# Streamed attention weights issued by GpSimd instead of SyncE, and the feed-forward bias added by an accumulating DMA

## The chip, the core and the metric

The kernel runs on one core of one Trainium2 chip. A core has TensorE (PE in the profile, with PEld for its weight loads), VectorE (DVE), ScalarE (ACT), GpSimd (POOL) and SyncE (SP). Each of them works through its own list of instructions in order. SP computes nothing here: it issues DMAs. ACT issues a few as well. The bytes of all of them are moved by the same 16 DMA engines of the core.

The metric is the device time of one execution in microseconds; lower is better.

## The reference

A "macaron" block works on x, 2 x 1024 tokens of 1024 float32 each: half a feed-forward network, attention, half a feed-forward network.

```python
x = x + 0.5 * ffn(layernorm(x), gate_w, base_w, base_b, lora_A, lora_B)
x = x + attn(layernorm(x), Wq, Wk, Wv, Wo)
x = x + 0.5 * ffn(layernorm(x), gate_w, base_w, base_b, lora_A, lora_B)

def ffn(x):                     # the same weights both times
    logits = x @ gate_w.T                      # 8 experts
    w, sel = top_k(logits, 2); w = softmax(w)
    result = x @ base_w.T + base_b             # 1024 -> 1024
    result += 2 * sum over the two experts of w * (x @ lora_A[e].T) @ lora_B[e].T   # rank 16
    return result

def attn(x):                    # 32 heads of 32, 8 key/value heads, RoPE, causal
    q, k, v = x @ Wq, x @ Wk, x @ Wv
    return softmax(mask(rope(q) @ rope(k).T / sqrt(32))) @ v @ Wo
```

What the change touches is `+ base_b` (scaled by 0.5, since half of the network's result is added) and the way in which Wq, Wk, Wv and Wo come to SBUF.

## The kernel before, in words

The 2048 tokens are 16 tiles of 128 (one token in a partition), 8 for each batch. A tile passes four stages: `stage_a1` (layernorm, first feed-forward network), `stage_a2` (projections to k and v, and to q in two halves), `stage_c1` (output projection after the attention, in two halves) and `stage_c2` (layernorm, second feed-forward network, store). Between a2 and c1 stands the attention: for each key/value head and each block of keys, `unit_s1` computes scores once for the row maximum, and `unit_s2` computes them again in transposed form, takes the exponential on ACT, and feeds the product with v and the row sums (`av_batch`).

All dense products split a float32 operand into two float16 halves and take three products for one (lines 358, 359 and 360, in `dense`). The feed-forward weights stay in SBUF (`wb`, `ag`). The attention's weights don't fit beside them: at the start they are scaled, split and written to DRAM (`wstr`, by `prep_stream`), five chunks (k and v together; q in two; o in two) of two halves, 1 MB each in the split form. From there every tile streams them in again. Three SBUF buffers `ws0` to `ws2` hold one half each. `prefetch(ci)`, called at the end of a dense product for the next chunk in the list `order`, issues the two loads of that chunk; half number n goes into the buffer that half number n - 3 has left, so it waits until the last matmul on half n - 3 has been done. In the kernel before, SP issues these loads at line 370. SP also issues the DMA transposes of the normalized rows (`tt`, line 314), of k (`kts`, line 501) and of q (`qt`, line 553), and loads and stores x.

In `ffn`, lines 393 to 395 add the bias to the residual tile `xt` in two halves of 512 columns on GpSimd. `xt` has been read by the layernorm's activation (line 349) at that time; the scaled result of the matmuls is added to it later, on DVE, half by half (line 444). The bias lies in SBUF in all 128 partitions (`bb`, loaded at line 793, halved on ACT at line 233).

GpSimd's other work: the variance's power -1/2 in `layernorm` (lines 335 and 337), products with the sine table in `rope` (475 and 479), the causal masks of the two kinds of score blocks (585 on `sm`, 720 on `p`), the low half of the attention's result (673), and in the preparation a quarter of the splitting (192) and small scalars (177, 187).

The order of the dense stages among the attention's units is written out by hand (`SEQS`, `NORMAL`, `plan`, `step`); the order of the instructions on every engine's list is then set by the framework's scheduler, which places an instruction by the time at which it reckons it ready. The instructions of one engine, DMA issues among them, start in that order.

Of the kernel before, what the change touches and what calls it, by code (L numbers as in the profile page):

```python
# [9 lines left out]
FP = mybir.dt.float32  # L10
# [3 lines left out]
ALU = mybir.AluOpType  # L14
AX = mybir.AxisListType

B, T, D = 2, 1024, 1024
NH, NKV, DH, GRP = 32, 8, 32, 4
E, R = 8, 16
P = 128  # L20
KB = D // P
# [18 lines left out]
def kernel(  # L40
# [16 lines left out]
    nc = tc.nc  # L57
# [3 lines left out]
    const = ctx.enter_context(tc.tile_pool(name="const", bufs=1))  # L61
    wres = ctx.enter_context(tc.tile_pool(name="wres", bufs=1))
    small = ctx.enter_context(tc.tile_pool(name="small", bufs=SB))
# [4 lines left out]
    dram = ctx.enter_context(tc.tile_pool(name="dram", bufs=1, space=bass.MemoryType.DRAM))  # L68
# [17 lines left out]
        out=cmask, in_=cmask, compare_op=ALU.is_ge, fill=-NEG, base=0,  # L86
# [6 lines left out]
        out=tri, in_=tri, compare_op=ALU.is_gt, fill=0.0, base=0,  # L93
# [7 lines left out]
    nc.gpsimd.memset(ones, 1.0)  # L101
    cosT = const.tile([P, TPB, DH // 2], FP)
    sinT = const.tile([P, TPB, DH], FP)
    bb = const.tile([P, D], FP)

    qst = [stat.tile([P, NH, P], HP, name=f"qst{j}") for j in range(2)]
    kst = stat.tile([P, NKV, P], HP)
# [9 lines left out]
    def pin(ins):  # L117

        if pinned[0]:
            tc.keep_in_program_order(ins)  # L120
# [3 lines left out]
    def load_x(t):  # L124
        xt = xp.tile([P, D], FP, name="xt")
        pin(nc.sync.dma_start(out=xt, in_=late["x"] if t == LATE and late else xf[bass.ts(t, P), :]))
        xts[t] = xt
# [8 lines left out]
    wstr = dram.tile([5, 2, P, 2, KB // 2, 512], HP)  # L136
# [88 lines left out]
    def prep_lora(st):  # L225
        c = const.tile([P, 2], FP, name="sl")
        nc.vector.tensor_copy(c[:, 0:1], S["l",])
        nc.vector.scalar_tensor_tensor(c[:, 1:2], INV["b", 0], S["l",], S["b", 1], ALU.mult, ALU.mult)
        for n in range(2):
            h, s = bass.ts(n, 512), c[:, n : n + 1]  # L230
            nc.scalar.activation(lbh[:, h], st[:, h], AF.Copy, scale=s)
            nc.vector.scalar_tensor_tensor(lbl[:, h], st[:, h], s, lbh[:, h], ALU.mult, ALU.subtract)
        nc.scalar.mul(bb, bb, 0.5)

    KV = [wk_in, wv_in]
    CHUNKS = {
# [8 lines left out]
    def stage(ci, h, slot, eng):  # L245
        staged[ci, h] = piece(slot, CHUNKS[ci][0], h, eng)
# [81 lines left out]
    def layernorm(xt, n=1):  # L328
        st = small.tile([P, 2, 6], FP, name="bst")
        for c in range(2):  # L330
            nc.vector.bn_stats(st[:, c, :], xt[:, bass.ts(c, 512)])
        mv = small.tile([P, 2], FP, name="mv")
        nc.vector.bn_aggr(mv, st.rearrange("p a b -> p (a b)"))
        ve = small.tile([P, 1], FP, name="ve")
        nc.gpsimd.tensor_scalar(ve, mv[:, 1:2], EPS, None, ALU.add)
        r = small.tile([P, 1], FP, name="r")
        nc.gpsimd.tensor_tensor(r, ve, mhalf, ALU.pow)
        n1 = small.tile([P, 1], FP, name="n1")
        nc.vector.scalar_tensor_tensor(n1, ve, r, r, ALU.mult, ALU.mult)
        nc.vector.tensor_scalar(n1, n1, -0.5 * XS, 1.5 * XS, ALU.mult, ALU.add)  # L340
        rs = small.tile([P, 1], FP, name="rs")
        nc.vector.tensor_tensor(rs, n1, r, ALU.mult)
        nb = small.tile([P, 1], FP, name="nb")
        nc.vector.scalar_tensor_tensor(nb, mv[:, 0:1], -1.0, rs, ALU.mult, ALU.mult)
        xn = fpool.tile([P, D], FP, name="xn")
        sp = Split(n)
        for i in range(n):
            c = bass.ts(i, D // n)
            nc.scalar.activation(xn[:, c], xt[:, c], AF.Identity, bias=nb, scale=rs)  # L349
            sp.add(xn)  # L350
        return sp

    def dense(ps, tt, wsel, n=512, last=True):

        for k in range(KB):
            wh, wl = wsel(k)
            th, tl = tt.high(k), tt.low(k)
            nc.tensor.matmul(ps, lhsT=th, rhs=wh, start=(k == 0), stop=False)  # L358
            nc.tensor.matmul(ps, lhsT=th, rhs=wl, start=False, stop=False)  # L359
            nc.tensor.matmul(ps, lhsT=tl, rhs=wh, start=False, stop=(last and k == KB - 1))  # L360
            if k % 2 == 1:
                yield
# [3 lines left out]
    def prefetch(ci):  # L366
        for h in range(2):
            w = wss[turn[0] % 3]
            turn[0] += 1
            nc.sync.dma_start(out=w, in_=wstr[ci, h])  # L370
            stream.append((ci, w))

    order = deque()
# [16 lines left out]
    def ffn(xt, tt, done):  # L390
        psa = p_dense.tile([P, 512], FP, name="pd")
        yield from dense(psa[:, 0 : P + E], tt, lambda k: (ag[:, 0, k, :], ag[:, 1, k, :]))
        for n in range(2):
            c = bass.ts(n, 512)
            nc.gpsimd.tensor_tensor(xt[:, c], xt[:, c], bb[:, c], ALU.add)  # L395

        lg = small.tile([P, E], FP, name="lg")
        nc.scalar.activation(lg, psa[:, P : P + E], AF.Copy, scale=S["cg"])
        nv = small.tile([P, 1], FP, name="nv")
        nc.vector.tensor_reduce(nv, lg, AX.X, ALU.max, negate=True)  # L400
        ex = small.tile([P, E], FP, name="ex")
        nc.scalar.activation(ex, lg, AF.Exp, bias=nv)
        fe = lg.unsqueeze(1).to_broadcast([P, E, E])
        ee = lg.unsqueeze(2).to_broadcast([P, E, E])
        lw = small.tile([P, E, R], FP, name="lw", bufs=1)
        gt, eq = lw[:, :, 0:E], lw[:, :, E : 2 * E]
        nc.vector.tensor_tensor(gt, fe, ee, ALU.is_gt)
        nc.vector.tensor_tensor(eq, fe, ee, ALU.is_equal)
        nc.vector.tensor_tensor(eq, eq, tri, ALU.mult)
        nc.vector.tensor_tensor(gt, gt, eq, ALU.add)  # L410
        rk = small.tile([P, E], FP, name="rk")
        nc.vector.tensor_reduce(rk, gt, AX.X, ALU.add)
        nc.vector.scalar_tensor_tensor(ex, rk, 1.5, ex, ALU.is_lt, ALU.mult)
        sm = small.tile([P, 1], FP, name="sm")
        nc.vector.tensor_reduce(sm, ex, AX.X, ALU.add)
        nc.vector.reciprocal(sm, sm)
        nc.vector.tensor_scalar(ex, ex, sm, S["inva2"], ALU.mult, ALU.mult)
        nc.vector.tensor_tensor(
            lw, psa[:, 0:P].rearrange("p (e r) -> p e r", r=R),
            ex.unsqueeze(2).to_broadcast([P, E, R]), ALU.mult,  # L420
        )
        yield True
        psb = [None, None]
        lh = ll = None
        for n in range(2):
            ps = p_dense.tile([P, 512], FP, name="pd")
            psb[n] = ps
            yield from dense(
                ps, tt, lambda k: (wb[:, n, 0, k, :], wb[:, n, 1, k, :]), last=False
            )  # L430
            if n == 0:
                pst = p_s1.tile([P, GRP, P], FP, name="s1")[:, 0, :]
                nc.tensor.transpose(pst, lw.rearrange("p e r -> p (e r)"), ident)
                lh = small.tile([P, P], HP, name="lh", bufs=LB)
                ll = small.tile([P, P], HP, name="ll", bufs=LB)
                nc.scalar.copy(lh, pst)
                nc.vector.tensor_tensor(ll, pst, lh, ALU.subtract)
                yield
            c = bass.ts(n, 512)
            nc.tensor.matmul(ps, lhsT=lh, rhs=lbh[:, c], start=False, stop=False)  # L440
            nc.tensor.matmul(ps, lhsT=lh, rhs=lbl[:, c], start=False, stop=False)
            nc.tensor.matmul(ps, lhsT=ll, rhs=lbh[:, c], start=False, stop=True)
            yield
            nc.vector.scalar_tensor_tensor(xt[:, c], ps, S["uf", n], xt[:, c], ALU.mult, ALU.add)  # L444
            done(n)
            if n == 0:
                yield True

    def stage_a1(t):
        tt = layernorm(xts[t])  # L450
        yield

        def done(n):
            if n == 1:
                Ts["x2", t] = layernorm(xts[t])
                if t == LATE:
                    late["x"] = dram.tile([P, D], FP, name="xlate")
                    nc.sync.dma_start(out=late["x"], in_=xts.pop(t))

        yield from ffn(xts[t], tt, done)  # L460
        yield True
# [310 lines left out]
    for h in range(2):  # L772
        for src, c in ((a_in, slice(0, P)), (g_in, slice(P, P + E))):
            pin(
                nc.sync.dma_start(
                    out=agst[:, h, :, c],
                    in_=src[h * (D // 2) : (h + 1) * (D // 2), :].rearrange("(k p) n -> p k n", p=P),
# [4 lines left out]
    pin(nc.sync.dma_start(out=lst, in_=lb_in))  # L782
    b0 = [piece(h - 2, [wb_in[:, 0:512]], h, nc.sync) for h in range(2)]
    load_x(1)
    a1 = [stage_a1(t) for t in range(3)]
    next(a1[0])
    prep_gate(gst)
# [2 lines left out]
    prep_base(0, b0)  # L790
    load_x(2)
    next(a1[1])
    pin(nc.sync.dma_start(out=bb, in_=bias_in.partition_broadcast(P)))
    stage(2, 0, 0, nc.scalar)
    stage(2, 1, 1, nc.scalar)
    prep_base(1, b1)
# [243 lines left out]
```

## Time and profile before

| | |
|---|---|
| median of 3 runs | 1523.7 us (1520.88 to 1530.89) |
| profiled execution | 1528.72 us, of which its span is 1527.0 us |
| granted TensorE clock, mean | 0.974 |
| PE busy | 1404.1 us, 92% of the span |
| DVE busy | 1139.7 us, 75% |
| ACT busy | 755.5 us, 49% |
| POOL busy | 450.1 us, 29% |
| DMA, mean | 175 GB/s |

The span runs from the first to the last instruction of the program. Busy times of engines overlap; a busy PE is not PE at its peak, because matmuls are pipelined and their ends are modelled. Issuing a DMA is not counted as busy time. A row of the form "SPq L370 <- PE pd L360: t, n, m" says that SP's queue stood at an instruction of line 370 and waited until a matmul of line 360 released it: t us in n times, at most m us. "To landing" is the time from the start of a DMA's issue until all its data is there.

### The profile page before, as it was taken

The numbers are of one execution on the slowest core, as the hardware profiler recorded it, in microseconds if no ns is written. First come the engines' busy times: TensorE is split into PE (matmuls) and PEld (weight loads), VectorE is DVE, ScalarE is ACT, GpSimd is POOL, SyncE is SP. The second block draws the span as 40 slices with busy tenths as digits, with TensorE's granted clock in tenths as the row PEclk, the third lists the DMA queues.
The fourth block names the chain that finished last, engine by engine and source line by source line (L and its number), as shares of the span: only waits on it lengthen the run. The fifth ranks groups of instructions, "written<-read, shape, count | busy, mean of one in ns | idle before, by whom it ended". The sixth has DMA issues, their size and how long they took to land.

```text
span 1527.0 us, 35303 instructions
## 1 busy us (share of the span) xinstructions
PE 1404.1 (92%) x14548; PEld 783.4 (51%) x14548; DVE 1139.7 (75%) x2420; ACT 755.5 (49%) x1374; POOL 450.1 (29%) x665
## 2 busy tenths in 40 slices
PE   3686897989999999999999899999999999989998
PEld 2243444455555555555654445555555555556544
DVE  6877656686968879789764767886869788689753
ACT  7564334453545545456552434553545455556631
POOL 3443213432323233122121323332323232312231
PEclk9798999989999999999999999999999999999999
DMA  9957697658575581853646769857383853834651
GB/s 274 333 156 204 115 237 205 206 127 264 123 238 137 153 254 31 235 160 69 209 160 191 216 161 272 202 160 234 72 294 69 237 147 70 271 69 98 133 170 45
DMA packets 293075, 267.30 MB, mean 175 GB/s; under 512 B 258480, under 2 KB 261552, under 8 KB 272432
## 3 DMA queue, kind: packets, MB, share of 16 engines
q1 hardware_dynamic: 289360, 252.45, 60.5%
q10 hardware_dynamic: 3552, 12.58, 2.3%
q8 instruction: 114, 1.87, 0.5%
q14 instruction: 49, 0.40, 0.1%
HBM read 181.63 MB, written 20.45 MB: 132 GB/s over the span
## 4 chain that ended last, share of the span: by engine, by line
PE 65%; DVE 13%; DMA 13%; ACT 3%; issue 2%; POOL 1%; SPq 1%; DVEq 0%; ACTq 0%; POOLq 0%
PE pd L358 13%; PE pd L359 13%; PE pd L360 13%; PE av L657 10%; PE s L712 7%; PE s L573 6%; DMA ws<-wstr 6%; DMA qt<-qst 5%; DVE mx L590 3%; DVE pair L636 1%; DVE ws L195 1%; DMA tt<-hl 1%; DVE o L666 1%; ACT p L718 1%; DVE hl L311 1%
## 5 line engine op out<-in xcount | busy, mean ns | idle before, releaser
L718 ACT ACTIVATE p<-s,cs 128x512 f32<-128x512 f32 x576 | 382.3, 688 | 291.2 <-PE s L712 284.1
L590 DVE TENSOR_REDUCE mx<-s 128x4 f32<-128x512 f32 x480 | 313.6, 675 | 68.3 <-PE s L573 46.8
L358 PE MATMUL pd<-ws,tt 128*128 128x512 f16 x592 | 226.8, 383 | 20.9 <-DMA ws<-wstr 16.8
L636 DVE TENSOR_TENSOR pair<-p,p 128x512 f32<-128x512 f32 x256 | 185.6, 727 | 72.6 <-ACT p L718 34.8
L573 PE MATMUL s<-kts,qt 96*128 96x128 f16 x2304 | 217.0, 222 | 23.8 <-DMA qt<-qst 17.8
L359 PE MATMUL pd<-ws,tt 128*128 128x512 f16 x592 | 226.3, 382 | 0.0
L712 PE MATMUL s<-qt,kts 128*128 128x512 f16 x576 | 210.7, 386 | 16.4 <-DMA qt<-qst 11.6
L360 PE MATMUL pd<-ws,tt 128*128 128x512 f16 x592 | 225.4, 382 | 0.0
L573 PEld LDWEIGHTS <-qt 96*128 96x128 f16 x2304 | 165.5, 99 | 116.4 <-issue 30.4
L359 PEld LDWEIGHTS <-tt 128*128 128x128 f16 x1360 | 135.6, 100 | 141.9 <-issue 31.3
L358 PEld LDWEIGHTS <-tt 128*128 128x128 f16 x1360 | 135.6, 100 | 135.5 <-issue 16.7
L358 PE MATMUL pd<-wb,tt 128*128 128x512 f16 x512 | 199.0, 389 | 5.0 <-DVE xt L444 5.0
L360 PEld LDWEIGHTS <-tt 128*128 128x128 f16 x1360 | 135.3, 99 | 131.5 <-issue 10.2
L359 PE MATMUL pd<-wb,tt 128*128 128x512 f16 x512 | 198.0, 387 | 0.5 <-DVE wb L195 0.5
L360 PE MATMUL pd<-wb,tt 128*128 128x512 f16 x512 | 197.7, 386 | 0.0
L657 PE MATMUL av<-p,va 128*32 128x128 f32 x4608 | 166.8, 278 | 4.8 <-ACT o L664 2.5
L720 POOL TENSOR_SCALAR_AFFINE_SELECT p<-p 128x512 f32<-128x512 f32 x128 | 89.0, 698 | 274.7 <-ACT p L718 264.4
L673 POOL TENSOR_TENSOR tt<-o,tt 128x128 f16<-128x128 f32 x128 | 70.5, 551 | 279.6 <-ACT tt L672 279.3
L657 PEld LDWEIGHTS av<-p,va 128*32 128x32 f32 x4608 | 115.5, 110 | 68.3 <-issue 53.4
L666 DVE RECIPROCAL o<-o 128x128 f32<-128x128 f32 x128 | 120.6, 942 | 24.9 <-ACT o L664 24.9
L585 POOL TENSOR_SCALAR_AFFINE_SELECT sm<-sm 128x512 f32<-128x512 f32 x96 | 66.4, 692 | 203.9 <-ACT sm L584 202.1
L395 POOL TENSOR_TENSOR xt<-xt,bb 128x512 f32<-128x512 f32 x64 | 92.3, 1464 | 59.6 <-ACT xn L349 59.4
(177 smaller groups left out, 1808.2 us busy)
## 6 DMA issues: line engine op xcount, KB each, us to landing
ws<-wstr SPq DMA_DIRECT2D x148, 1024.0 KB, 5.9
wstr<-ws ACTq DMA_DIRECT2D x9, 1024.0 KB, 6.1
xt<-in_x_dram SPq DMA_DIRECT2D x16, 512.0 KB, 3.8
out_dram<-xt SPq DMA_DIRECT2D x15, 512.0 KB, 2.8
ws<-in_wb_dram SPq DMA_DIRECT2D x2, 1024.0 KB, 8.0
qst<-in_wb_dram SPq DMA_DIRECT2D x2, 1024.0 KB, 6.8
st<-in_wo_dram SPq DMA_DIRECT2D x2, 1024.0 KB, 10.0
kts<-in_wo_dram SPq DMA_DIRECT2D x2, 1024.0 KB, 12.0
```

Source lines behind the costliest of these rows:

```text
L358: nc.tensor.matmul(ps, lhsT=th, rhs=wh, start=(k == 0), stop=False)
L359: nc.tensor.matmul(ps, lhsT=th, rhs=wl, start=False, stop=False)
L360: nc.tensor.matmul(ps, lhsT=tl, rhs=wh, start=False, stop=(last and k == KB - 1))
L395: nc.gpsimd.tensor_tensor(xt[:, c], xt[:, c], bb[:, c], ALU.add)
L573: nc.tensor.matmul(ps[:, h, :], lhsT=q[0 : 3 * DH, h, :], rhs=KT[b0 + j][0 : 3 * DH, g, :], start=(not pem or h == 0), stop=not pem,)
L590: nc.vector.tensor_reduce(mx[:, odd, j, :], ps, AX.X, ALU.max)
L636: nc.vector.tensor_tensor(sums, us[i][1], us[i + 1][1], ALU.add)
L657: prev = nc.tensor.matmul(av[rows, i, :], lhsT=w, rhs=p32[:, h, :], start=(us[0][0] == 0 and n == 0), stop=(last and n == len(runs) - 1), ...
L666: nc.vector.reciprocal(rc, rc)
L712: ins = nc.tensor.matmul(ps.rearrange("p h k -> p (h k)"), lhsT=KT[b0 + j][:, g, :], rhs=q.rearrange("p h k -> p (h k)"), start=True, stop ...
L718: nc.scalar.activation(p32, ps, AF.Exp, scale=cs)
L720: nc.gpsimd.affine_select(out=p32, in_=p32, compare_op=ALU.is_ge, fill=0.0, base=0, pattern=[[0, GRP], [1, P]], channel_multiplier=-1,)
```

## The change

There are two edits.

1. The 148 loads at line 370 (368 in the changed file) are issued by GpSimd and not by SP. Sources, buffers and their number stay as they are.
2. The bias is no longer kept in SBUF in 128 partitions. 4 KB of it are loaded as 128 rows of 8 numbers (`hs`), halved on GpSimd, and written back to DRAM (`hb`). In `ffn`, the two GpSimd additions give way to one DMA issued by GpSimd that reads `hb` once for each of the 128 partitions and adds it to `xt` while it writes. The load of `bb` and its halving on ACT go.

```diff
-    bb = const.tile([P, D], FP)
...
-        nc.scalar.mul(bb, bb, 0.5)
...
     def prefetch(ci):
         for h in range(2):
             w = wss[turn[0] % 3]
             turn[0] += 1
-            nc.sync.dma_start(out=w, in_=wstr[ci, h])
+            nc.gpsimd.dma_start(out=w, in_=wstr[ci, h])
             stream.append((ci, w))
...
     def ffn(xt, tt, done):
         psa = p_dense.tile([P, 512], FP, name="pd")
         yield from dense(psa[:, 0 : P + E], tt, lambda k: (ag[:, 0, k, :], ag[:, 1, k, :]))
-        for n in range(2):
-            c = bass.ts(n, 512)
-            nc.gpsimd.tensor_tensor(xt[:, c], xt[:, c], bb[:, c], ALU.add)
+        nc.gpsimd.dma_start(out=xt, in_=hb.partition_broadcast(P), accum_op=ALU.add)
...
     load_x(1)
+    hs = small.tile([P, KB], FP, name="hs", bufs=1)
+    pin(nc.sync.dma_start(out=hs, in_=bias_in.rearrange("(p k) -> p k", k=KB)))
+    nc.gpsimd.tensor_scalar(hs, hs, 0.5, 0.0, ALU.mult, ALU.add)
+    hb = dram.tile([D], FP, name="hb")
+    nc.gpsimd.dma_start(out=hb.rearrange("(p k) -> p k", k=KB), in_=hs)
     a1 = [stage_a1(t) for t in range(3)]
...
     next(a1[1])
-    pin(nc.sync.dma_start(out=bb, in_=bias_in.partition_broadcast(P)))
```

## The prediction

> **What bounds the kernel now.** First the page's busy shares, then the table by stages.
>
> ```profile
> span 1527.0 us, 35303 instructions
> ## 1 busy us (share of the span) xinstructions
> PE 1404.1 (92%) x14548; PEld 783.4 (51%) x14548; DVE 1139.7 (75%) x2420; ACT 755.5 (49%) x1374; POOL 450.1 (29%) x665
> ...
> 500.00:700.00 200.00, 196.50 (x2375) 115.76 (x2373) 167.20 (x336) 111.25 (x198) 57.69 (x79) 1.00 0.56 159
> 900.00:1100.00 200.00, 187.47 (x1894) 104.68 (x1894) 153.34 (x329) 99.66 (x185) 68.11 (x101) 0.99 0.71 185
> ```
>
> A stage's row begins with its length; then come PE, PEld, DVE, ACT and POOL busy, granted clock, DMA share, GB/s. PE is the bound: it idles 3.5 us of 200 in one stage and 12.5 in the other. By the same table it idles 54 us before 160 us (preparation) and 69 after. So a gain after 160 us can't pass 69 us, and what delays PE is paid in full. Next, what PE waited for after 160 us, and the loads at line 370:
>
> ```profile
> PE pd L358 <- DMA ws<-wstr: 16.8, 15, 2.2
> PE s L712 <- DMA qt<-qst: 11.6, 12, 2.1
> PE s L573 <- DMA qt<-qst: 9.3, 8, 2.4
> ...
> L370 SPq DMA_DIRECT2D ws<-wstr x148: 319/320/2036, 133.1 to 1484.1; - x148
> ...
> DMA to landing us min/median/max: 4.7/5.9/10.9
> ```
>
> PE lost 16.8 us to streamed weights and 20.9 to transposed q, both issued by SP. Then SP's own waits and one tile's stretch of its timeline (start, time, merged issues):
>
> ```profile
> SPq L553 <- DVE qst L603: 206.8, 28, 22.1
> SPq L370 <- PE pd L360: 190.6, 65, 11.0
> ...
> 433.79 3.35 SPq L370 DMA_DIRECT2D ws<-wstr  x2
> 438.16 1.24 SPq L553 DMA_TRANSPOSE qt<-qst  x1
> 439.63 0.40 SPq L370 DMA_DIRECT2D ws<-wstr  x1
> 440.32 1.51 SPq L501 DMA_TRANSPOSE kts<-kst  x1
> 444.33 11.41 SPq L370 DMA_DIRECT2D ws<-wstr  x4
> ```
>
> SP mostly stands ready at a load before its buffer is free. Matching load n with the matmuls on half n - 3 (which free its buffer) and on half n (which use it), three quarters of the loads go out 0.03 us after the buffer is free. What is left between landing and use is small: at most 0.2 us in 22 of 148, under 2 us in 46, under 4 in 78. The seven loads issued in the rows above had 2.7, 2.4, 0.2, 1.7, 1.8, 5.9 and 3.2 us. The stream has latency to spare, but little.
>
> **The change, step by step.**
>
> *Loads, latency.* 148 loads leave SP for POOL's queue. Let each land d us later after its buffer is free. A late use frees the next buffer late, so the shift is carried: use n shifts by the larger of the shift of use n - 1 and (shift of use n - 3) + d - (spare time of load n). For the tile above with d = 2, the load with 0.2 spare shifts its use by 1.8; later loads absorb the next d, and the tile pays 1.8 us once. Over all 148 loads the last use shifts by 7 us for d = 0.5, 15 for 1, 25 for 1.5, 35 for 2, 59 for 3. I use the spare times of before because the order of PE's list keeps them: by the changed list, PE's own work between freeing and next use of a buffer has a median of 9.6 us, as before.
>
> d isn't in the trace: no DMA is issued by POOL there. Nearest row: the fastest tenth of the loads from SP lands within 4.8 us. The Trainium skill ("DMA: Bandwidth & Descriptors") gives two prices for a 1 MB load issued from GpSimd. Its fit (Anatomy of one DMA) makes 2.0 + 1.05 MB/436 GB/s = 4.4 us, thus d = -0.4, costing nothing. Its table (Measured) has 6.15 us of transfer with descriptor writing left out; with its 1 us to the first byte about 7.2, thus d = +2.3, about 42 us. The same page (Issuing engines are not separate DMA queues) says that issuing from more engines saves issue time alone, and this issue takes 0.32 us on SP; that speaks against the change. I take 1.5, between them and nearer the table, which is for this size: **+25** (0 to 59).
>
> *Loads, starved descriptors.* A rule speaks against the change outright: the Trainium skill ("SBUF — State Buffer", Who interferes with whom) says that GpSimd can't write descriptors while DVE is in a mode that takes both ports, and to issue from SP or ACT instead. The row: the operations named there (copy, cast, tensor_scalar, all in SBUF) are 128x1 things of 0.15 us on this DVE; its time goes to reductions from PSUM (L590, 313.6 us busy) and two-input additions (L636, 185.6), which that page doesn't count as such. By the rule read strictly, half a 0.7 us operation in 75% of cases would add 0.26 us to d, some 5 us; by the row 0. I take **0** (0 to 5).
>
> *Loads, POOL's order.* POOL works in order, so a load can stand behind work that isn't ready, and work behind a load whose buffer isn't free. SP waited 357 us at line 370 in all (seven rows of its waits, 190.6 the largest). In the changed POOL list I compared where, in PE's list, the matmul that frees each buffer stands, and the score matmul of each of the 128 masks at 720: only 3 masks stand behind a load that is freed after their own scores. Loads don't stand behind masks that come later than their buffer either, but do stand behind some that come at about that time. Laying this list over the times of before, at 1 us of POOL per DMA (an estimate), a load goes out 0.5 us later in the mean and 2.2 in the worst tenth. By the carried shift that is 9 more; since the real times move along, I take **+5** (0 to 12). POOL gains some 181 us for 181 DMAs and loses 92, so it stays near 540 us, 35%: not a bound.
>
> *SP relieved.* The 128 qt transposes don't queue behind waiting loads. Of the 64 that follow the maximum (line 603), 13 went out over 1 us late, 7 of them directly behind a load. About half of PE's 20.9 us: **-10** (-21 to 0). What is late next is the maximum itself: SP's largest wait is for line 603.
>
> *Additions removed.*
>
> ```profile
> L395 POOL TENSOR_TENSOR xt<-xt,bb 128x512 f32<-128x512 f32 x64 | 92.3, 1464 | 59.6 <-ACT xn L349 59.4
> ...
> bb<-in_bias_dram SPq DMA_DIRECT2D x1, 512.0 KB, 4.9
> ```
>
> 64 additions go; POOL isn't the bound and nothing waited for them directly. DVE operations that ran beside them (L311, L636 and others) took 15 us longer in all than their medians; DVE has 25% to spare. **-1** (-3 to 0).
>
> *Accumulating DMAs added.* 32 of 512 KB each, reading the same 4 KB for every partition as the load of bb did in 4.9 us. An addition also reads its destination; with no such row I bound landing by 4.9 and 10 us. The first DVE addition at 444 comes 20 to 90 us after the bias addition's start, except in the preparation (4.7 us, where bb itself was late), so this is hidden; if cover fell below 10 us, each shortfall would hold a PSUM buffer and PE. In POOL's list 11 of the 32 stand right ahead of a load and take DMA time from it: 11 x 4.9 us through the same spare times, **+3** (0 to 6).
>
> *Preparation.* `hs` queues behind 2 MB of base weights; `hb` is written and must land before the first accumulation. In POOL's list that one stands ahead of the power at 177 which starts the base weights' scale:
>
> ```profile
> 20.09 0.55 POOL L177 TENSOR_TENSOR ar<-ar,half 128x1 f32<-128x1 f32 x1 [0.53 <-DVE n L340]
> ```
>
> Base weights were being measured from 13.8 us and x arrived by 16.1, so hs is there at about 16.5, the write at about 20 to 21 (a small gw load took 4.2 us to land here), and the power starts near 22: **+2** (0 to 6). The bb load and its 1.05 us on ACT go, beside a DMA share near 1.0; nothing more.
>
> Sum: 25 + 0 + 5 - 10 - 1 + 3 + 2 = **+24 us**. Against the profiled execution's own time, 1528.7 becomes 1552.7. The profiled run lies 5 us above the median of the runs shown; on that median, 1523.7 becomes **1547.7**, 1.6% slower.
>
> **Rivals.** A measurement of this kernel tells about 1% from no change.
>
> *Faster: one ring becomes two.* Before, loads and transposes shared SP's queue, and a load waited behind a transpose ahead of it: 5.9 us median against 4.8 for the fastest. If POOL's loads pass the transposes and land in 4.8 to 5.9, d is at most 0 and the SP relief remains: 16.8 + 20.9 us of PE waits, two thirds of them gone, about 1500. For it: the landings of 7 to 9 us where transposes are dense. Against it: many of those are two loads behind one another, which stays. It decides from d below about 0.5, where 7 us of shift no longer outweigh 10 of relief.
>
> *Cancelled.* d near 0.8 costs 11, relief gives 10: about 1527.
>
> *POOL jams.* If POOL stands in its queue as SP did, masks come late. Laid over the times of before, 16 of 128 p masks come over 4 us late; beyond 3 us of cover this sums to 97 us. If half reached PE through DVE's pair sums, +48 on top of 24: about 1596. Against it: the 3 in 128 above.
>
> *Slower bias.* If the accumulation landed after its cover, PE would wait 32 times; at 10 us it stays covered.
>
> **How the numbers follow.** Forecast (slower by 1 to 4%) 0.55; jam or d of 3 and more, 0.09; cancelled 0.24; two rings 0.12. The forecast's own ends: d of 1 gives 1538, d of 2.5 with a late preparation 1575. For eight in ten I reach down to most of the two-rings case, 1508, and up to the jam, 1598. Slower by over 1% (above 1538.9) takes the forecast and the jam, less a little of the forecast's low end: 0.62. Faster (below 1508.5) most of two rings: 0.11. Within: 0.27.
>
> **What would show it.** Loads from POOL landing 1 to 2 us later than 5.9 us and PE's wait for ws rising from 16.8 to 40 us or more; PE's wait for qt near 10; POOL's masks with DVE waiting not much more than before (14 us); no DVE wait for xt at 444; PE's first matmul on wb at about 25 us and not 23.1. I am wrong if loads land within 5.9 us (two rings), or if PE waits for av or DVE for masks grow by tens of us (jam).

## The result, and the profile after

The changed kernel takes **1646.43 us** (median of 4 runs, 1620.07 to 1654.03) against 1525.18 us before, measured on the same chip (4 runs, 1520.88 to 1530.89). The ratio is 1.0715, 95% interval 1.0659 to 1.0771: slower by 7%, and outside the predicted range. The ratio counts only the runs within 1.5% of the fastest (1620.07 and 1642.63 us), so it is below that of the two medians, and the profiled execution, 1650.22 us, is not among them. Its span is 121.5 us longer than before. What is read from it stands in the profiles of the loads alone (1668.19 us) and of the loads on ACT too, shown below.

The head of the page and the queues:

```profile
span 1648.5 us, 35381 instructions
## 1 busy us (share of the span) xinstructions
PE 1429.0 (87%) x14548; PEld 795.1 (48%) x14548; DVE 1121.9 (68%) x2420; ACT 753.2 (46%) x1373; POOL 463.4 (28%) x783
...
q0 software_dynamic: 25952, 171.98, 35.6%
q1 hardware_dynamic: 268048, 96.73, 34.3%
```

TensorE (PE) is busy 24.9 us longer (before 1404.1) and so idle 96.6 us longer: together the whole 121.5 us. The busy part is clock: the mean granted clock fell from 0.974 to 0.942, and the same weight matmuls take 397 ns in the mean and not 383. First the row of before, then that of after:

```profile
L358 PE MATMUL pd<-ws,tt 128*128 128x512 f16 x592 | 226.8, 383 | 20.9 <-DMA ws<-wstr 16.8
L356 PE MATMUL pd<-ws,tt 128*128 128x512 f16 x592 | 235.3, 397 | 75.6 <-DMA ws<-wstr 70.0
```

The clock is low in the stretches where PE stands (0.82 in the row of 395 to 440 us below). Over the ten profiles of the block in this document it goes with PE's idle time: 0.971 to 0.974 where PE idles 98 to 123 us, 0.953 to 0.961 at 161 to 193, 0.941 to 0.942 at 220 to 243. So this part seems to follow from the waits. POOL is busy for 28%: not a bound. The loads have left q1 for q0. A queue of this kind, in which one issuing engine's DMAs stand, is called a ring below: q1 is SP's, q0 POOL's, q10 ACT's. The bytes of all still pass the same 16 DMA engines.

PE's waits over the whole run show where the idle time is (total us, times, longest). First two rows of before, then those of after:

```profile
PE s L573 <- DMA qt<-qst: 17.8, 10, 5.7
PE pd L358 <- DMA tt<-hl: 6.1, 5, 2.1
```


```profile
PE pd L356 <- DMA ws<-wstr: 70.0, 18, 17.6
PE s L569 <- DMA qt<-qst: 61.7, 11, 15.6
PE pd L356 <- DMA tt<-hl: 17.3, 9, 4.4
...
PE s L708 <- DMA qt<-qst: 3.6, 6, 1.2
...
PE av L653 <- POOL p L716: 2.8, 3, 2.2
```

(All numbers of lines are 2 to 4 lower than before: 370 is 368, 553 is 549.) Weights: 70.0 us, before 16.8. Transposed queries: 65.3, before 29.4 (17.8 and 11.6; the prediction's 20.9 leaves out what came before 160 us). Transposed activations: 17.3, before 6.1. These three rose by 100.3 us, slightly more than the whole new idle time. It is PE waiting for DMAs, and *both* sides got worse: the loads that moved to POOL and the transposes that stayed with SP. The landings (issue to landing: min, median, max), first by the loads' line, then by the queries':

```profile
L368 POOL DMA_DIRECT2D ws<-wstr x148: 527/577/850, 127.7 to 1597.5; - x148
...
DMA to landing us min/median/max: 4.9/6.6/33.9
```

```profile
L549 SPq DMA_TRANSPOSE qt<-qst x128: 1231/1248/11996, 127.9 to 1565.7; - x128
DMA to landing us min/median/max: 2.7/4.3/36.3
```

Before, the landings of the queries were

```profile
DMA to landing us min/median/max: 3.0/3.9/16.4
```

and those of the loads stand in the prediction. The medians hardly moved (5.9 to 6.6, 3.9 to 4.3). The tail did: before, no load took over 11 us; now 34 do, 19 take over 15, and the longest 33.9. The mean landing of a load rose from 6.27 to 9.02 us, the mean of its fastest three quarters only from 5.60 to 6.35. So the loss is not a delay of every load but some disasters. The table by stages shows one of them; a row holds start and end, length, PE, PEld, DVE, ACT and POOL busy, granted clock, DMA share, GB/s:

```profile
395.00:440.00 45.00, 28.21 (x267) 15.56 (x266) 21.35 (x38) 14.09 (x24) 9.93 (x16) 0.82 1.14 132
404.00:416.00 12.00, 12.00 (x117) 6.79 (x115) 9.06 (x15) 5.03 (x11) 3.72 (x6) 1.00 1.23 58
```

The same query on before, for the burst of the same kinds of DMA that the prediction showed by its timeline:

```profile
433.00:470.00 37.00, 37.00 (x378) 20.56 (x375) 25.53 (x58) 16.60 (x33) 8.75 (x15) 1.00 0.94 294
```

In the second row of after, the DMA share (the packets' time in flight, added up, over that of 16 engines) is 1.23, and 58 GB/s come out. Before, with a share of 0.94, it was 294. There is no lack of packets: they take long. SP's timeline in that window (start, length, instructions):

```profile
393.66 6.54 SPq L549 DMA_TRANSPOSE qt<-qst  x3
402.74 32.41 SPq L312 DMA_TRANSPOSE tt<-hl  x1
```

The issue of one transpose of activations held SP for 32.4 us. Read from the trace, the transposes issued at 395.0 and 398.7 us landed after 21.8 and 36.3 us, and the loads issued by POOL at 395.2, 399.8 and 403.9 after 18.3, 33.3 and 33.9. Other such groups lie at 205, 483, 581, 906, 1005 and 1314 us, among more; those at 483, 581 and 1314 have no accumulating DMA near. Each holds DMA transposes in q1 together with loads in q0.

Which came first is telling. Of the 148 loads, 79 went out while a DMA transpose was in flight (issued and not yet landed), and all 34 that took over 11 us are among these. Of the other 69, into which a transpose may have come later, none took over 10.3. Before, in one ring, 67 loads went out behind a transpose in flight, and the longest took 10.9.

### The profile page after: what moved, and what is told of

Its sections match the earlier page's. It is cut to its first block, busy times and chain, and to the rows that moved or that the text cites. A ratio compares the mean times of both kernels' runs of the same rounds, so it can differ in the third digit from the quotient of the medians.

```text
span 1648.5 us, 35381 instructions
## 1 busy us (share of the span) xinstructions
PE 1429.0 (87%) x14548; PEld 795.1 (48%) x14548; DVE 1121.9 (68%) x2420; ACT 753.2 (46%) x1373; POOL 463.4 (28%) x783
## 3 DMA queue, kind: packets, MB, share of 16 engines
q1 hardware_dynamic: 268048, 96.73, 34.3%
## 4 chain that ended last, share of the span: by engine, by line
PE 61%; DMA 23%; DVE 7%; issue 4%; ACT 3%; POOL 2%; SPq 0%; ACTq 0%; POOLq 0%; DVEq 0%
PE pd L356 12%; PE pd L357 11%; PE pd L358 11%; PE av L653 11%; DMA ws<-wstr 10%; DMA tt<-hl 7%; PE s L569 6%; PE s L708 6%; DMA qt<-qst 4%; DVE mx L586 1%; ACT p L714 1%; DMA xt<-in_x_dram 1%; DVE ws L194 1%; PE pd L436 1%; DVE hl L309 1%
## 5 line engine op out<-in xcount | busy, mean ns | idle before, releaser
L356 PE MATMUL pd<-ws,tt 128*128 128x512 f16 x592 | 235.3, 397 | 75.6 <-DMA ws<-wstr 70.0
L569 PE MATMUL s<-kts,qt 96*128 96x128 f16 x2304 | 220.9, 225 | 65.4 <-DMA qt<-qst 61.7
L569 PEld LDWEIGHTS <-qt 96*128 96x128 f16 x2304 | 168.8, 100 | 160.2 <-DMA qt<-qst 66.5
L357 PE MATMUL pd<-ws,tt 128*128 128x512 f16 x592 | 234.3, 396 | 0.0
L358 PE MATMUL pd<-ws,tt 128*128 128x512 f16 x592 | 233.2, 394 | 0.0
L357 PEld LDWEIGHTS <-tt 128*128 128x128 f16 x1360 | 137.3, 101 | 191.0 <-issue 86.1
L632 DVE TENSOR_TENSOR pair<-p,p 128x512 f32<-128x512 f32 x256 | 181.8, 713 | 64.9 <-PE av L653 29.1
L356 PEld LDWEIGHTS <-tt 128*128 128x128 f16 x1360 | 137.3, 101 | 160.5 <-issue 23.4
L358 PEld LDWEIGHTS <-tt 128*128 128x128 f16 x1360 | 137.4, 101 | 138.7 <-issue 22.3
L368 POOL DMA_DIRECT2D ws<-wstr x148 | 85.4, 577 | 358.6 <-PE pd L358 187.0
L669 POOL TENSOR_TENSOR tt<-o,tt 128x128 f16<-128x128 f32 x128 | 63.0, 492 | 208.4 <-ACT tt L668 208.0
```

The source lines that it names most:

```text
L368: nc.gpsimd.dma_start(out=w, in_=wstr[ci, h])
L569: nc.tensor.matmul(ps[:, h, :], lhsT=q[0 : 3 * DH, h, :], rhs=KT[b0 + j][0 : 3 * DH, g, :], start=(not pem or h == 0), stop=not pem,)
L632: nc.vector.tensor_tensor(sums, us[i][1], us[i + 1][1], ALU.add)
```

## The experiments

Theory A: loads in a second ring and DMA transposes in SP's ring slow each other. Rivals: B, GpSimd's software ring is slow by itself; C, the accumulating DMAs clog it. All kernels of the block are the one before with the edit shown, except where said.

### Each half of the change alone

```diff
# e1_loads: the loads' edit alone
-            nc.sync.dma_start(out=w, in_=wstr[ci, h])
+            nc.gpsimd.dma_start(out=w, in_=wstr[ci, h])
```

> Only the first edit: the 148 loads issued by GpSimd, the bias added on GpSimd as before. Theory A (streamed loads in a second ring and DMA transposes in SP's ring slow each other down): nearly all of the loss is here, 1600 to 1640 us, loads landing at up to 15 us and more, PE waiting over 50 us each for ws and for qt. Theory C (the accumulating DMA clogs the ring in which the loads stand): 1530 to 1555 us, loads landing near 6 us. The prediction's sum for this edit alone: 1524 + 25 + 5 - 10 = 1544 us.

`e2_bias` is the changed kernel with that one line put back to `nc.sync`.

> Only the second edit: the bias by accumulating DMAs from GpSimd, the loads on SP as before. Theory A: since the 32 accumulations are small and few, 1525 to 1545 us. Theory C: 1590 us and more, with loads or transposes landing late around each accumulation. The prediction's sum for this edit alone: 1524 + 3 + 2 - 1 = 1528 us.

Measured: the loads alone take **1680.11 us** (median of 1658.16, 1668.19, 1692.02 and 1693.9). Counted as for the ratio above it is 1663 us, 142 more than before (1520.86), and this figure is used in the differences below. Every one of the four runs is above the 1600 to 1640 expected by theory A. The bias alone takes **1518.35 us** (ratio 0.998, interval 0.9966 to 0.9994). In the profile of the loads alone PE waits for the same things as in the changed kernel:

```profile
PE pd L358 <- DMA ws<-wstr: 68.3, 18, 10.4
PE s L573 <- DMA qt<-qst: 47.5, 12, 12.1
PE s L712 <- DMA qt<-qst: 32.5, 12, 9.7
PE pd L358 <- DMA tt<-hl: 18.0, 5, 11.7
```

The order is as in the changed kernel: 77 loads went out with a transpose in flight, 34 of them took over 11 us; of the other 71 the longest took 7.9. The accumulating DMAs of the bias alone, by their line:

```profile
L391 POOL DMA_DIRECT2D xt<-hb x32: 890/955/955, 19.7 to 1491.6; - x32
...
who waited for it (us, times):
...
DMA to landing us min/median/max: 5.2/7.3/14.3
```

The list of who waited is empty. So the whole loss belongs to the loads' edit, C falls, and the bias's edit is worth a gain of about 3 us (1 to 5 by the interval). The kernel with the bias's edit alone beats both kernels, barely (by 0.2%), and is the fastest here of those that leave nothing out. Why both edits together lose less than the loads alone (1620 to 1654 against 1658 to 1694) was not settled.

### A second ring that the hardware serves

```diff
# e3_act
-            nc.sync.dma_start(out=w, in_=wstr[ci, h])
+            nc.scalar.dma_start(out=w, in_=wstr[ci, h])
```

> The kernel before with the streamed loads issued on ACT's queue, a second ring that the hardware serves, and nothing else changed. ACT now waits for free weight buffers, so its time alone says little; what counts is how the loads and the transposes land. Theory A: as in the loads-on-GpSimd kernel, a share of the loads and of the transposes beside them lands 15 to 35 us after issue, transposes' packets of 256 bytes take over 100 ns in those stretches, and the time is over 1600 us. Theory B: loads land within 13 us as before, transposes of qt in 4 to 5 us with a longest below 15, and the time is 1520 to 1560 us, by ACT's waits alone.

Measured: **1663.29 us**, ratio 1.0915 (1.0876 to 1.0954). Its loads and PE's waits:

```profile
L370 ACTq DMA_DIRECT2D ws<-wstr x148: 326/326/346, 132.2 to 1620.5; - x148
...
DMA to landing us min/median/max: 4.7/6.3/24.9
```

```profile
PE pd L358 <- DMA ws<-wstr: 81.0, 17, 10.6
PE s L573 <- DMA qt<-qst: 43.9, 12, 11.6
PE pd L358 <- DMA tt<-hl: 24.1, 6, 13.0
PE s L712 <- DMA qt<-qst: 18.1, 12, 9.2
```

It is the picture of the loads on POOL, with nearly the same time (1663 us), in a ring that the profile lists as hardware_dynamic (q10) where POOL's q0 is software_dynamic: 28 loads land after more than 15 us, queries after up to 31.9. Of the 78 loads that went out with a transpose in flight 41 took over 11 us; of the other 70 the longest took 7.5. B falls: both second rings that were tried do it.

### Rings by themselves, first two attempts

The first kernel of DMAs alone was meant to run stages of transposes and loads, one after the other.

> Nothing of the reference is computed: 17 stages one after the other, each of 4 transposes (128x2048 float16, SP), 4 loads (1 MB) or 4 accumulating DMAs (512 KB), alone or together. Every stage is read from its first issue to its last landing. Alone: transposes 18 us, loads 19 us from any queue. Theory A: transposes beside loads from ACT's queue and beside loads from GpSimd's queue both take well over the sum of 37 us (50 and more), on SP's queue alone about 37. Theory B (it is GpSimd's software-written descriptors, not the second ring): only beside GpSimd's loads is it over 45 us. No interference: 37 us in all three. If one packet of each ring is taken in turn, loads in pieces of 512 bytes instead of 8 KB let the transposes land earlier.

Its join between the stages looked at one tile only, so later stages ran into earlier ones. It gave no answer on rings, only the duration of packets (in the median 309 ns for 8 KB and 18 ns for 256 bytes). The second had a join over all tiles. Its core, with the stages that matter:

```python
def join():                                     # every tile is read, then written from the maximum
    for j, t in enumerate(every): nc.vector.tensor_copy(seen[:, j : j + 1], flat(t)[:, 0:1])
    nc.vector.tensor_reduce(g, seen, AX.X, ALU.max)
    for t in every + [src]: nc.vector.tensor_scalar(flat(t)[:, 0:1], g, 0.0, None, ALU.mult)
PHASES = [ [(transpose, 8)], [(load on SP, 4)], [(load on ACT, 4)], [(load on POOL, 4)],
  [(transpose, 8), (load on SP, 4)], [(transpose, 8), (load on ACT, 4)], [(transpose, 8), (load on POOL, 4)],
  ... [(copy, 8)], [(copy, 8), (load on SP, 4)], [(copy, 8), (load on POOL, 4)], ... ]
```

> Seventeen stages with a full join between them, in a kernel that does nothing else (the macaron block is left out). Stages: 8 DMA transposes of 128x2048 fp16 alone (SP's ring); 4 loads of 1 MB alone in SP's, ACT's and GpSimd's ring; the 8 transposes with the 4 loads in SP's, ACT's, GpSimd's ring; 8 smaller transposes (128x1024) alone and with the loads in each of the three rings; 8 SBUF-to-SBUF copies in 256-byte pieces alone, with loads in SP's and in GpSimd's ring; 4 accumulating DMAs of 512 KB alone and beside 8 transposes; the transposes with GpSimd's loads again. Theory A (two rings with DMA transposes in one of them slow each other): transposes with ACT's loads and with GpSimd's loads both take over 1.3 times the sum of the two alone, with packets of 256 bytes at 100 ns and more; in SP's one ring the stage takes no more than the sum. Theory B (only GpSimd's software-written ring does it): ACT's stage is as SP's, GpSimd's alone is over 1.3 times the sum. Theory D (two rings don't disturb each other by themselves; what slows them in the big kernel is something else that runs there): all three stages take the sum of the two alone or less.

Measured, from the first issue of a stage to its last landing: 8 transposes alone 21.8 us; 4 loads alone 12.3 (SP), 13.1 (ACT), 12.7 (POOL); both together 36.0 us in SP's one ring, but 31.3 with the loads in ACT's ring and 31.6 in POOL's. Theory D then, at first sight: two rings cost nothing here. But the order of landing says something. In the stage with POOL's loads, the first transpose, issued at 0.7 us, landed at 15.0, when all four loads were in. Counted per microsecond in the middle of it:

```
us of the trace   8 KB packets (q0)   256-byte packets (q1)   GB/s
173.0 to 174.0    54, 309 ns each     51, 18 ns each          455
174.0 to 175.0    48, 309 ns          64, 18 ns               410
175.0 to 176.0    48, 309 ns          49, 18 ns               406
```

The packets of the two rings come in nearly equal numbers, as if taken in turn. A transpose of 512 KB is 2048 packets of 256 bytes, so beside 8 KB packets it crawls. It costs the transposes their turn, and no throughput: not what the big kernel shows. In this stage the four loads went out at 0.0, 0.5, 1.0 and 1.6 us, one behind the other, and the first load was running when the first transpose came. No other stage of this kernel (smaller transposes, copies, accumulating DMAs) took more than the sum of its parts alone.

### Transposes or small packets

The block again, with every DMA transpose replaced by a plain copy of as many bytes, cut into the same 256-byte pieces, on the same queue at the same place.

```diff
# e4_copy_sp; e5_copy_pool is the same with the loads on nc.gpsimd
+    def blocks(to, src):
+        return nc.sync.dma_start(out=to, in_=src.unsqueeze(1).to_broadcast([P, to.shape[1], P]))
-        nc.sync.dma_start_transpose(out=kt, in_=ks.rearrange("p g c -> p (g c)"))
+        blocks(kt, ks[:, NKV - 1, :])
...                     # tt and qt in the same way, each from the piece of its source that is written last
-            nc.scalar.activation(p32, ps, AF.Exp, scale=cs)
+            nc.scalar.activation(p32, ps, AF.Exp, scale=0.0)
```

> The kernel before with every DMA transpose (tt, qt, kts) replaced by a plain SBUF-to-SBUF copy of as many bytes in pieces of 256 bytes on the same queue at the same place; the transposition and the exponential's scale are left out (scale 0), so the output is not the reference's. Loads stay in SP's ring. All theories: within 3% of the kernel before, 1480 to 1560 us; it is the base for the next one.

> The same kernel with copies for transposes (transposition and the exponential's scale left out), and the streamed loads on GpSimd's queue. Theory A1 (it is the transposition that cannot stand a second ring): within 2% of e4_copy_sp, loads landing within 13 us. Theory A2 (any stream of 256-byte packets in one ring beside 8 KB packets in another): 5 to 10% slower than e4_copy_sp, with loads landing up to 30 us. Theory B (GpSimd's software ring is slow by itself in this kernel): 5 to 10% slower too, but with the copies landing as fast as in e4_copy_sp and only the loads late.

Measured: **1499.47 us** with the loads on SP (1495.06 to 1500.84), **1513.4 us** with the loads on POOL (1507.84 to 1513.71). Moving the loads now costs 13.9 us, 0.9%, where with transposes it cost 142 (1663 against 1520.86). PE's waits with the loads on POOL:

```profile
PE s L572 <- DMA qt<-qst: 19.2, 5, 6.6
PE s L711 <- DMA qt<-qst: 12.1, 7, 4.1
...
PE pd L359 <- DMA ws<-wstr: 6.7, 8, 1.7
```

and its loads:

```profile
L371 POOL DMA_DIRECT2D ws<-wstr x148: 530/576/773, 130.7 to 1470.6; - x148
...
DMA to landing us min/median/max: 5.0/6.1/9.4
```

All loads land within 9.4 us, also the 77 that went out with a copy in flight, with the same instruction on the same queue, among nearly as many 256-byte packets of another ring (264976 in q1, against 268048 with transposes). So neither POOL's queue nor small packets make the disasters: transposition does (A1). One difference stays untested: a copy reads one 256-byte piece of each partition over and over, a transpose its whole source. What is left fits the turn-taking: PE's wait for queries rises from 8.2 us (loads on SP) to 31.3, their longest landing from 9.0 to 15.3.

### The order of arrival

The DMA kernel once more, with loads held back by a fill of a 2 MB tile on their own engine, so that they arrive some 4 us apart, while transposes are under way. (The first load of a stage, on ACT the first two, is not held: its fill had run before.)

```diff
# m3_order, against the second DMA kernel
+    def late(i, eng):
+        tc.keep_in_program_order(nc.gpsimd.memset(scr, 0.0))      # on ACT: a copy
+        load(i, eng)
```

> Eleven stages, the block left out. Here the transposes run first and the 1 MB loads arrive while they are in flight: each load follows a filling of a 2 MB tile on its own engine. Stages: 8 transposes (128x2048) alone; 4 such loads on GpSimd's queue alone; both; both with ACT's queue; 256-byte copies for the transposes with GpSimd's loads; 8 smaller transposes with the loads; both sizes of transposes with the loads; then transposes with VectorE additions and matmuls beside them, without loads, with GpSimd's loads, copies in their place, and all in SP's ring. Theory A1-order (a load that arrives in a second ring while transposes are under way stalls both): the stage of both moves under 100 GB/s over some us, packets of 256 bytes take over 100 ns there, and it lasts over 1.3 times the transposes' 21.8 us plus 10 us; copies in their place don't. Theory A1-work (compute engines' traffic has to come on top): the same only in the stage with work. Theory turn (the DMA engines only take packets of the two rings in turn, one of each): no stage longer than the sum, only the transposes late, with as many 256-byte as 8 KB packets per us while loads are there.

Measured, first issue to last landing:

```
stage                                                     us   PE and DVE beside it
8 transposes alone                                      22.8   work
4 held loads on POOL alone                              17.3   work
both                                                    40.3   work
both, loads on ACT                                      42.7   work in part
256-byte copies for the transposes, loads on POOL       32.2   DVE only
8 transposes alone, again                               22.3   none
both, again                                             40.1   none
copies and held loads on POOL, again                    32.1   none
transposes and loads (not held) in SP's ring            35.6   none
```

The last four stages were meant to have work of PE and DVE beside them, and the first ones none. It came out the other way round: nothing held that work back, so it ran ahead, as the columns of PE and DVE show. Two stages with smaller transposes are left out of the table; in them, too, loads landed late (after up to 17.1 us).

The stage of both with POOL's loads is from 88.5 to 128.8 us, that with copies from 183.4 to 215.6, each with its middle in the row below it; the last row is "both, again" (columns as above):

```profile
88.50:128.80 40.30, 40.30 (x188) 18.29 (x187) 26.27 (x55) 0.00 (x0) 15.94 (x8) 1.00 1.11 209
104.00:116.00 12.00, 12.00 (x57) 5.48 (x56) 3.64 (x5) 0.00 (x0) 0.44 (x1) 1.00 1.32 118
183.40:215.60 32.20, 0.00 (x0) 0.00 (x0) 24.47 (x63) 0.00 (x0) 15.96 (x8) 0.50 1.08 261
187.00:203.00 16.00, 0.00 (x0) 0.00 (x0) 9.55 (x11) 0.00 (x0) 13.11 (x7) 0.50 1.06 337
347.30:387.40 40.10, 0.00 (x0) 0.00 (x0) 2.91 (x35) 0.00 (x0) 15.96 (x8) 0.50 1.10 209
```

This is the disaster in the small: a DMA share of 1.32 with 118 GB/s, down to 25 in single microseconds, where copies move 337 under the same loads. The length of 40.3 us alone would prove nothing, since it is the sum of the two stages by themselves (22.8 and 17.3); the copies, which take 32.2, show what the overlap could have been. The packets beside one another:

```
us of the trace   8 KB packets        256-byte packets       GB/s
both, 110 to 111  3                   44, 472 ns each        36
both, 113 to 114  15, 312 ns each     84, 169 ns             144
copies, 193-194   49, 318 ns          48, 19 ns              414
```

A 256-byte packet of a transpose takes some 20 times as long as one of a copy in the worst microsecond, and the longest 8 KB packet 6.3 us instead of 1.1. The work of other engines makes no difference (40.3 with it, 40.1 without; copies 32.1 without), nor does the engine that issues the loads (42.7): A1-order holds. The second DMA kernel shows that a transpose in flight is not enough: there two of the four loads went out after the first transpose as well, but close behind loads of their own ring, and the transposes cost nothing but their turn. Whether it matters that the ring of the loads runs empty in between, or how the loads are spaced, was not separated.

### Which transposes, and the size of a packet

```diff
# loads on nc.gpsimd; e6_qt_copy: only the 128 transposes of queries become copies
-        nc.sync.dma_start_transpose(out=q, ...)
+        blocks(q, QS[t][:, (g + 2) * GRP - 1, :])
# e7_rest_copy: only the 48 of activations and the 16 of keys become copies
# e8_2k: all transposes stay; a load is 512 packets of 2 KB
-    wstr = dram.tile([5, 2, P, 2, KB // 2, 512], HP)
+    wstr = dram.tile([5, 2, 4, P, 1024], HP)
```

> Loads on GpSimd's queue, and only the 128 transposes of queries (qt) replaced by copies in 256-byte pieces; the transposes of tt and kts stay (the queries' transposition and the exponential's scale are left out). If the many small qt transposes are what collides: 1500 to 1540 us. If any transposes do, by the bytes that they move (128 x 256 KB of qt against 48 x 512 KB and 16 x 256 KB of the others, 32 MB against 28 MB), about half of the 9% stays: 1560 to 1610 us, and loads landing after more than 15 us are about half as many as the 23 of the kernel with loads alone moved.

> Loads on GpSimd's queue, and the transposes of tt and kts replaced by copies in 256-byte pieces; the 128 transposes of qt stay (the other transpositions and the exponential's scale are left out). If the larger bursts of tt and kts are what collides: 1500 to 1540 us. If any transposes do, by bytes: 1560 to 1620 us, with the loads landing late near qt transposes alone.

> The kernel with the loads alone moved to GpSimd's queue, and the weights' DRAM copy laid out so that a load consists of 512 packets of 2 KB, not 128 of 8 KB. Theory turn (the DMA engines take one packet of each ring in turn, so that a 256-byte packet waits for an 8 KB one): a transpose now gets through four times as fast beside a load, and the time falls below 1590 us, with few transposes over 15 us. Theory A1 (transposes and a second ring stall each other whatever the packet): 1640 us or more, and loads and transposes landing as late as before.

Measured: 1576.33 us with only tt and kts transposed (ratio to before 1.0358, 1.0307 to 1.041), 1588.72 us with only the queries transposed (1.044, 1.0287 to 1.0592), 1614.9 us with 2 KB packets (1.0612, 1.0536 to 1.0687). Each family of transposes brings its part, 63 and 75 us above the 1513 with none, near their shares of bytes; together with both it is 150 (1663 less 1513). Loads over 15 us are 7 and 7, against 23 with all transposes, where half of them had been expected for the first. Smaller packets help some: 14 such loads, and 48 us less than the loads alone moved. That is neither of the two expectations (under 1590 or over 1640), so the size of the other ring's packets is part of the price and not all of it. The kernel with 2 KB packets differs in its loads' issue too (0.77 us on POOL and not 0.58).

What makes a transpose's packets wait inside the DMA engines for those of another ring was not found, and no run here looks into them.

## Why the prediction was wrong

*What bounds the kernel* was right: PE, with little spare time between the landing of a weight half and its use. What delays PE was paid in full, and the fall of the clock on top of it (+24.9 us of busy PE, for which the sum had no term).

**Two steps failed, *Loads, latency* (+25) and *SP relieved* (-10), and for one reason:** both took it that loads in one ring and transposes in another don't slow each other. In the profiled execution PE's waits grew by 53 us for ws, by 36 for qt where 10 of relief were forecast, and by 11 for tt, for which the sum had no term.

*Loads, latency* (with d = 1.5) gave every load the same added landing time. The trace of after has +0.8 in the median and +2.75 in the mean, mostly from a tail of 19 loads in 148 between 15 and 34 us. Put through the prediction's own carried shift, d = 2.75 gives 52 us, about what was measured; but with each load's own rise the shift comes to 90, so that agreement is in part luck. The 1.5 was chosen between two prices of the Trainium skill for a load from GpSimd ("DMA: Bandwidth & Descriptors", Anatomy of one DMA and Measured), both of them for a load by itself. By itself it costs little: 12.7 us for four from POOL against 12.3 from SP, and 6.1 against 5.8 us in the median where copies run beside it (e5 and e4), so d was 0.3. What the step lacked was a term for the other ring's transposes. The trace of before had one such meeting, in the preparation: a query's transpose went out at 135.0 us, ACT's stores of 1 MB to `wstr` (q10) at 135.5 and 138.4. The transpose landed after 16.4 us, the longest of its kind, and the stores after 12.8 each, the longest of theirs; the same two stores took 6.8 and 6.3 us with the loads alone moved, where the transposes had landed before, and 4.0 and 4.7 beside no transposes at all (e4).

*SP relieved* (-10) has the wrong sign and is the largest miss, 46 us. The queries no longer stand behind waiting loads, but PE's wait for them rose from 29.4 to 65.3 us. Even where nothing collides (e5) it rose by 23 us, which fits packets of two rings taken in turn. The queue in SP had been protection: a load that waits behind a transpose in one ring took at most 10.9 us.

*Starved descriptors* (0) stands: the ring of ACT, q10, which the profile lists as hardware_dynamic, loses as much (1.0915). The page of the Trainium skill weighed there ("SBUF — State Buffer", Who interferes with whom) advises to issue from SP or ACT instead; in this kernel ACT is no better than POOL, so the stall that this page describes does not account for the loss.

*POOL's order* (+5) was at most that. Loads go out 0.3 us after their buffer is free in the median, 0.6 in the mean (before 0.03 and 0.9). DVE's waits for the masks did grow by tens of us, the sign that the prediction had named for a jam: sm and p together from 29.9 us to 55.0 in the changed kernel, and to 48.7 with the loads alone moved. But they are 56.5 with the loads on ACT, where none stands on POOL, and 20.5 with the loads on POOL and copies for transposes (e5), against 27.4 with them on SP (e4). So they come with the collisions and not from the loads' place on POOL, and PE's own wait for the p masks stayed small (2.8 us, before 2.1). The rival "POOL jams" falls.

*Additions removed, accumulating DMAs, preparation* (-1, +3, +2): together +4 predicted, about -3 measured (ratio 0.998). The DMAs land in 5.2 to 14.3 us, wider than the 4.9 to 10 assumed, under a cover of 20 to 90; in the changed kernel one took 34.5, inside the group of 395 us, and still nothing waited for it. The first matmul on wb came at 23.4 us, not at 25. The preparation did slip later: the last of the first eight splits of wb on DVE began at 34.5 us and not 27.4 (35.2 with the bias alone), and the bias alone was no slower for it.

*The rivals.* "One ring becomes two" named the right object and drew the wrong sign from it. The range ended at 1598 because the worst mechanism in it was POOL's order. That the forecast had said slower at all was luck: it had the direction from added latency that a load by itself hardly has. None of the cases was one in which both sides get slower.

## What to carry to other kernels

Before moving DMAs to another queue, ask what runs beside them there that the old queue kept apart: a queue's order is also a guard, and its waits in the profile may be cheaper than what they prevent. Where DMA transposes and large loads came in the same stretch here, one ring was better; if a kernel with two rings is slow, look for a DMA share above 1 with few GB/s, and at the longest landing, not the median. Look in the profile before, too, for a single case of the meeting that the change will make common: here two stores and a transpose of the preparation showed it. An estimate of landing time that gives all transfers the same number can't see a collision: price the transfer beside its neighbours, by a small kernel that lets one arrive while the other runs.

## What the runs showed of the hardware that was not expected

- Loads of 1 MB that arrive in a second ring while DMA transposes are under way in the first can stall both: 40.3 us for work that takes 32.2 with copies of the same packets; 256-byte packets up to 472 ns in the mean of a microsecond instead of 18 to 25. It is the same with the loads in ACT's ring (42.7).
- The order counts: in three kernels of the block all 109 loads over 11 us went out with a transpose in flight in the other ring; the 210 loads that did not go out so took 10.3 us at most. (With packets of 2 KB it is 28 of 29, and the other took 11.0.)
- Packets of two rings were taken about one for one: beside 8 KB packets the 256-byte ones of the other ring moved at some 50 per us, against 750 per us alone (16384 in 21.8 us).
- One ring with eight transposes and four loads takes 36.0 us, a little over the sum of the two alone (21.8 and 12.3).
- A 4 KB packet of an accumulating DMA takes as long as a plain one of 8 KB (344 ns in the mean against 325), so half the rate: four of 512 KB took 13.0 us, as long as four plain loads of 1 MB.
